# Layer 2 of a fused graph network: the pairs ordered by a list scheduler instead of hand-written steps

## The chip, the cores and the metric

One core of one Trainium2 chip runs the whole network in one launch. The metric is the device time of that launch in microseconds (us). The engines are named as in the profile: PE is the matmul engine and PEld its weight loads, DVE the vector engine, ACT the engine of activation functions, POOL the general-purpose engine, SP the queue that issues most DMA transfers.

## The reference, cut to what matters

Four graph layers run one after the other over 2708 nodes of 128 features with one dense 2708 x 2708 matrix `adj`. The change is in layer 2, which works on points of a hyperbolic ball:

```python
local_t = logmap(h[:, None, :], h[None, :, :])          # a vector for every pair i, j
scores = (h_t @ att_wl)[:, None] + (h_t @ att_wr)[None, :] + att_b[0]
adj_att = sigmoid(scores) * adj
support_t = jnp.einsum('ij,ijd->id', adj_att, local_t)  # sum over j
h = proj(expmap(support_t, h))
h = relu(logmap0(h))
x = _layernorm(x + proj(expmap0(h)))
```

`logmap` of a pair is a scalar factor times a fixed combination of the two points, so what must be made for every pair is one number: with a Gram product of the two points giving minus the hyperbolic cosine, less one, of their distance, the factor is the distance over its hyperbolic sine. This factor is the same for (i, j) and (j, i). It is multiplied by the sigmoid of the score and by `adj`, and the result is summed over j by matmuls.

## The kernel before, in words

Layers 0 and 1 come first, then layer 2's preparation, its stage of the pairs, its end, and layer 3. The change is inside the stage of the pairs.

The nodes are 22 tiles of 128 (the last has 20 rows), split in two halves of 11 tiles (`HT`). A `Pair` is one tile of neighbours j (the partitions) against one half of the nodes i (the columns: 1408 in half 0, 1300 in half 1). There are 44: `A` (half 0 with tiles of half 0), `B` (half 0 with tiles of half 1), `C` (half 1 with tiles of half 1), `D_` (half 1 with tiles of half 0). Since the factor is symmetric, A and C pairs work out only the columns from their own tile on (`dw` of them, "direct") and get the rest (`mw`) as transposes of earlier pairs' results, "mirrors". B pairs are all direct, and each stores its result in a DRAM table `f_tab`; D pairs are all mirrors, read from that table.

For a pair, the work on each engine is:

- PE: `gram` (L1386 in float32 and L1387 in bfloat16, up to 512 columns into one PSUM bank `ps`); `mirror` (L1449, transposes of 128 columns into a bank); `add_up` (L1464 into `accV`, three banks, and L1466 into `accO`, one bank).
- ACT: `clear` (L1396, relu out of the bank), `square` (L1400), `root` (L1404), `log` (L1414), `gate` (L1418, sigmoid). Root, logarithm and sigmoid lie in different function tables; each change of table is an ACT_TABLE_LOAD. Relu, square and copy run under any of them.
- DVE: `sinh` (L1407), `exp_d` (L1410), `over_sinh` (L1426), `gated_adj` (L1422), `times_f` (L1433), and the product with a mirror (L1450), each over the pair's columns.
- SP: `load` of the tile of `adj` (L1369), the store to `f_tab` (L1429), `load_f` from it (L1380 and L1381). POOL clears the diagonal (L1372).

All intermediate tiles lie in one `arena` of 264 cells of 128 columns. `taken` and `released` assign them in the order in which the program is written; a tile that is written into cells still being read waits for the reader. The four remaining PSUM banks rotate through one pool, `pg`, for grams and mirrors alike.

The instruction order on every engine is the written order (`tc.manual_schedule`). It comes from 14 hand-chosen `steps` of two to five pairs. In one step, in this order, the roots of the pairs `now`, the mirrors and last products of the pairs `done` (the step before), the first `add_up` and up to four clears of the pairs `after`, sinh and exp of `now`, the other add-ups alternating with the remaining grams and clears, then the logarithms, `gated_adj`, the loads and gates of `after`, `over_sinh`, and `load_f`. The first two grams of the step after next are placed at the end:

```python
for v in direct(now):
    v.log()
for v in now:
    v.gated_adj()
...
coming = [(v, a, b) for v in direct(at_step(step + 2)) for a, b in v.direct]
early = [v.gram(a, b) for v, a, b in coming[:2]]
```

After the last pair of a half, `accV` and `accO` are copied out by DVE and ACT in turn (L1478, L1479); the first half's sums are parked in DRAM (`v_tab`). Then the end of layer 2 and layer 3 start: transposes of the sums (L1623), and layer 3's matmuls over `adj` (L1726).

Of the kernel before, what the change touches and what calls it, by code (L numbers as in the profile page):

```python
# [35 lines left out]
def spans(start, stop, step):  # L36
    return [(a, min(a + step, stop)) for a in range(start, stop, step)]


@with_exitstack  # L40
def gnn_stack(ctx: ExitStack, tc: tile.TileContext, t, out: bass.AP):
# [975 lines left out]
    def layers_1_to_3(top, before_end=lambda: None):  # L1017
# [144 lines left out]
        with ExitStack() as l2:  # L1162
# [146 lines left out]
            with ExitStack() as att:  # L1309
                CELLS = 264  # L1310
                arena = att.enter_context(tc.tile_pool(name="arena", bufs=1)).tile([P, CELLS * P], F32, name="arena")
                pacc = att.enter_context(tc.tile_pool(name="ps_acc2", bufs=1, space=PSUM))
                pg = att.enter_context(tc.tile_pool(name="ps_g", bufs=4, space=PSUM))
                free = {k: -1 for k in range(CELLS)}
                clock = itertools.count()

                def taken(width):

                    n, runs = -(-width // P), []
                    for k in sorted(free):  # L1320
                        if runs and runs[-1][-1] == k - 1:
                            runs[-1].append(k)
                        else:
                            runs.append([k])
                    fits = [(len(r), max(free[k] for k in own), own[0]) for r in runs if len(r) >= n
                            for own in (r[:n], r[-n:])]
                    at = min(fits)[2]
                    for k in range(at, at + n):
                        del free[k]
                    return at  # L1330

                def released(cells):
                    free.update(dict.fromkeys(cells, next(clock)))

                class Pair:
# [4 lines left out]
                    def __init__(self, hf, j):  # L1340
                        self.hf, self.j, self.r = hf, j, rows[j]
                        self.c0, self.c1 = halves[hf]
                        self.w = self.c1 - self.c0
                        self.js = slice(j * P, j * P + self.r)
                        self.own_half = self.c0 <= j * P < self.c1
                        self.first = j - hf * HT if self.own_half else 0

                        self.mw = self.first * P if self.own_half else self.w if hf else 0
                        self.dw = self.w - self.mw
                        self.cells = {}  # L1350
                        self.direct, self.mirrors = spans(0, self.dw, BANK), spans(0, self.mw, BANK)
                        Pair.of[hf, j] = self

                    def new(self, name, width):
                        at = taken(width)
                        self.cells[name] = set(range(at, at + -(-width // P)))
                        return arena[:self.r, at * P:at * P + width]

                    def drop(self, name):
                        released(self.cells.pop(name))  # L1360

                    def drop_column(self, k):
                        cell = max(self.cells["f"]) - (HT - 1 - k)
                        self.cells["f"].discard(cell)
                        released([cell])

                    def load(self):
                        self.at = self.new("at", self.w)
                        nc.sync.dma_start(out=self.at, in_=adjT[self.js, self.c0:self.c1])  # L1369
                        if self.own_half:  # L1370
                            d = self.at[:, self.mw:self.mw + self.r]
                            nc.gpsimd.tensor_mul(d, d, off[:self.r, :self.r])  # L1372

                    def load_f(self):
                        if self.dw == 0:
                            at = taken(HW)
                            self.cells["f"] = set(range(at, at + HT))
                            f = self.fT = arena[:, at * P:at * P + HW].rearrange("p (k c) -> p k c", c=P)
                            k = HT - 1
                            nc.sync.dma_start(out=f[:, :k, :], in_=f_tab[:k, :, self.js].rearrange("k p c -> p k c"))  # L1380
                            nc.sync.dma_start(out=f[:rows[-1], k, :], in_=f_tab[k, :rows[-1], self.js])  # L1381

                    def gram(self, a, b):
                        ps = self.ps = pg.tile([P, BANK], F32, name="ps")[:self.r, :b - a]
                        c = slice(self.c0 + self.mw + a, self.c0 + self.mw + b)
                        nc.tensor.matmul(ps, XT[:, self.js], XT[:, c], start=True, stop=False)  # L1386
                        nc.tensor.matmul(ps, aux[0][:, self.js], aux[1][:, c], start=False, stop=True)  # L1387
                        return ps

                    def clear(self, a, b, ps, on_vector):  # L1390
                        if a == 0:
                            self.m = self.new("m", self.dw)
                        if on_vector:
                            nc.vector.tensor_scalar(self.m[:, a:b], ps, -1.0, 0.0, op0=ALU.mult, op1=ALU.max)
                        else:
                            nc.scalar.activation(self.m[:, a:b], ps, AF.Relu, scale=-1.0)  # L1396

                    def square(self):
                        self.u = self.new("u", self.dw)
                        nc.scalar.activation(self.u, self.m, AF.Square, bias=1.0)  # L1400

                    def root(self):
                        self.f = self.new("f", self.dw)
# [5 lines left out]
                    def exp_d(self):  # L1409
                        nc.vector.scalar_tensor_tensor(self.u, self.m, 1.0, self.u, op0=ALU.add, op1=ALU.add)  # L1410
                        self.drop("m")
# [4 lines left out]
                    def gate(self):  # L1416
                        self.w_ = self.new("w", self.w)
# [3 lines left out]
                    def gated_adj(self):  # L1421
                        nc.vector.tensor_mul(self.w_, self.w_, self.at)  # L1422
                        self.drop("at")

                    def over_sinh(self):
                        nc.vector.scalar_tensor_tensor(self.f, self.u, DMAX, self.f, op0=ALU.min, op1=ALU.mult)  # L1426
                        self.drop("u")
                        if not self.own_half:
                            nc.sync.dma_start(out=f_tab[self.j - HT, :self.r, :], in_=self.f)  # L1429

                    def times_f(self):
                        v = self.w_[:, self.mw:]
                        nc.vector.tensor_mul(v, v, self.f)  # L1433
                        if self.own_half:
# [4 lines left out]
                    def mirror(self, a, b):  # L1439
                        ps = pg.tile([P, BANK], F32, name="ps")[:self.r, :b - a]  # L1440
                        for c in range(a, b, P):
# [7 lines left out]
                            nc.tensor.transpose(ps[:, c - a:c - a + n], src, ident[:n, :n])  # L1449
                        nc.vector.tensor_tensor(self.w_[:, a:b], self.w_[:, a:b], ps, op=ALU.mult)  # L1450
                        if b == self.mw and self.own_half:
                            for k in range(self.first):
                                Pair.of[self.hf, self.hf * HT + k].drop_column(self.first)
                        elif b == self.mw:
                            self.drop("f")

                    def add_up(self, first, last):
                        if first:
                            Pair.acc = (pacc.tile([P, 3 * BANK], F32, name="accV"),
                                        pacc.tile([P, BANK], F32, name="accO"))  # L1460
                        accV, accO = Pair.acc
                        pieces = spans(0, self.w, BANK)
                        for a, b in pieces:
                            nc.tensor.matmul(accV[:, a:b], X[:self.r, self.j, :], self.w_[:, a:b], start=first, stop=last)  # L1464
                        for k, (a, b) in enumerate(pieces):
                            nc.tensor.matmul(accO[32 * k:32 * k + 1, :b - a], X0[:self.r, self.j:self.j + 1],  # L1466
                                             self.w_[:, a:b], start=first, stop=last)
                        self.drop("w")
                        if last:
                            if self.hf:  # L1470
                                VT = VT1
                            else:
                                at = taken(self.w)
                                VT = arena[:, at * P:at * P + self.w]
                                released(range(at, at + HT))
                            for k, (a, b) in enumerate(pieces):
                                copy = nc.scalar.copy if k % 2 else nc.vector.tensor_copy
                                copy(VT[:, a:b], accV[:, a:b])  # L1478
                                copy(V0T[32 * k:32 * k + 1, self.hf, :b - a], accO[32 * k:32 * k + 1, :b - a])  # L1479
                            if self.hf == 0:  # L1480
                                nc.sync.dma_start(out=v_tab, in_=VT)

                A, B = [Pair(0, j) for j in range(HT)], [Pair(0, j) for j in range(HT, NT)]
                C, D_ = [Pair(1, j) for j in range(HT, NT)], [Pair(1, j) for j in range(HT)]
                steps = [A[:2], A[2:5], A[5:7] + B[:1], A[7:8] + B[1:3], A[8:9] + B[3:5], A[9:10] + B[5:7],
                         A[10:] + B[7:9], B[9:], C[:2] + D_[:1], C[2:4] + D_[1:3], C[4:6] + D_[3:5], C[6:8] + D_[5:7],
                         C[8:] + D_[7:9], D_[9:]]
                order = [v for s in steps for v in s]
                assert len(order) == 2 * NT

                def direct(vs):
                    return [v for v in vs if v.dw]

                def at_step(n):
                    return steps[n] if 0 <= n < len(steps) else []

                with tc.manual_schedule():
                    early = []
                    for step in range(-1, len(steps) + 1):
                        now, after, done = at_step(step), at_step(step + 1), at_step(step - 1)  # L1500
                        adds = [functools.partial(v.add_up, n % NT == 0, n % NT == NT - 1)
                                for n, v in enumerate(order) if v in done]
# [326 lines left out]
```

## Time and profile before

| | |
|---|---|
| median of 3 runs | 1919.74 us (1918.43 to 1920.09) |
| the profiled execution | 1919.87 us, of which the span of instructions is 1918.0 us |
| PE busy over the span | 1620.9 us (85%) |
| DVE | 1441.5 us (75%) |
| ACT | 1041.9 us (54%) |
| POOL | 624.7 us (33%) |
| mean granted PE clock over the span | 0.919 |
| stage of the pairs | 1242.6 to 1620.0 us |
| in it: PE, DVE, ACT busy | 301.5, 252.6, 245.1 us of 377.4 us |
| in it: granted PE clock | 0.84 |

The busy times are sums over instructions; PE's are modelled and grow when the granted clock falls, so they are not an amount of work. In the lists of waits a line gives the engine and the line that waited, what it waited for, the total, the number of times and the longest. In the timeline a line gives start, duration, engine, line, output and inputs, count, and in brackets the idle time before it and what ended it. `arena` stands for every tile in the arena, so the line number tells which operation is meant.

### The profile page before, as it was taken

The numbers are of one execution on the slowest core, as the hardware profiler recorded it, in microseconds if no ns is written. First come the engines' busy times: TensorE is split into PE (matmuls) and PEld (weight loads), VectorE is DVE, ScalarE is ACT, GpSimd is POOL, SyncE is SP. The second block draws the span as 40 slices with busy tenths as digits, with TensorE's granted clock in tenths as the row PEclk, the third lists the DMA queues.
The fourth block names the chain that finished last, engine by engine and source line by source line (L and its number), as shares of the span: only waits on it lengthen the run. The fifth ranks groups of instructions, "written<-read, shape, count | busy, mean of one in ns | idle before, by whom it ended". The sixth has DMA issues, their size and how long they took to land.

```text
span 1918.0 us, 36613 instructions
## 1 busy us (share of the span) xinstructions
PE 1620.9 (85%) x14033; PEld 960.8 (50%) x14033; DVE 1441.5 (75%) x3615; ACT 1041.9 (54%) x1528; POOL 624.7 (33%) x426
## 2 busy tenths in 40 slices
PE   5899999999999999885699996678776888199995
PEld 5666666666666666664444443423222443044542
DVE  7899999999999999986588885757777764860104
ACT  3666667667666766654344443587777640440003
POOL 5667757766766776664100000000000000000000
PEclk8899999999999999997799998778897879599998
DMA  8756666665766666443044410022334543454331
GB/s 212 164 118 145 130 142 131 137 138 128 147 121 141 140 135 143 91 99 114 1 150 146 167 70 1 22 85 104 137 108 143 167 142 125 184 203 145 143 123 31
DMA packets 234896, 238.30 MB, mean 124 GB/s; under 512 B 28844, under 2 KB 219630, under 8 KB 228122
## 3 DMA queue, kind: packets, MB, share of 16 engines
q1 hardware_dynamic: 183670, 212.18, 35.7%
q0 software_dynamic: 51040, 23.68, 10.5%
q8 instruction: 112, 1.84, 0.4%
q14 instruction: 74, 0.61, 0.1%
HBM read 220.65 MB, written 15.15 MB: 123 GB/s over the span
## 4 chain that ended last, share of the span: by engine, by line
PE 41%; DVE 29%; POOL 8%; DMA 8%; issue 7%; ACT 6%; SPq 0%; DVEq 0%; ACTq 0%; POOLq 0%
PE acc L1726 10%; POOL far L782 8%; PE accV L1464 6%; PE lg L1099 5%; PE acc L1106 5%; DVE ix L778 5%; DMA far<-d_tab,ix 4%; DVE W L883 3%; DVE extra L796 2%; PE ps L1386 2%; PE accO L1466 2%; DVE o L740 2%; PE sl L818 2%; DVE S L708 2%; DVE dA L701 2%
## 5 line engine op out<-in xcount | busy, mean ns | idle before, releaser
L782 POOL DMA_INDIRECT far<-d_tab,ix x352 | 562.2, 1597 | 257.6 <-DVE W L883 112.1
L896 ACT ACTIVATE g<-sl 128x768 f32<-128x768 f32 x484 | 392.9, 812 | 257.9 <-PE sl L823 207.9
L818 PE MATMUL sl<-dA,S 124*128 124x153 f16 x4840 | 408.2, 232 | 10.4 <-DVE W L883 7.7
L818 PEld LDWEIGHTS <-S 124*128 124x128 f16 x4840 | 330.5, 98 | 79.8 <-issue 68.2
L834 PE MATMUL acc<-g,W 128*32 128x128 f32 x4840 | 205.5, 277 | 0.5 <-issue 0.5
L834 PEld LDWEIGHTS acc<-g,W 128*32 128x32 f32 x4840 | 140.6, 109 | 58.7 <-issue 55.5
L823 PE MATMUL sl<-s,same 50*128 50x384 f16 x968 | 161.9, 308 | 0.0
L883 DVE TENSOR_TENSOR W<-sl,own 128x150 f32<-128x150 f32 x484 | 143.2, 300 | 14.1 <-ACT g L896 13.5
L1464 PE MATMUL accV<-arena,X 128*128 128x512 f32 (+4 forms) x264 | 130.4, 636 | 20.9 <-DVE arena L1450 11.8
L1100 ACT ACTIVATE w<-lg,row_L_gnn_gate_bias 128x512 f32<-128x512 f32 (+1 forms) x132 | 83.4, 636 | 108.2 <-PE lg L1099 107.0
L708 DVE TENSOR_SCALAR S<-rk 124x1000 f16<-124x1000 bf16 (+1 forms) x330 | 133.9, 431 | 0.0
L778 DVE FIND_INDEX8 ix<-v,o 128x8 uint32<-128x2728 f32 x44 | 131.7, 2994 | 0.0
L1372 POOL TENSOR_TENSOR arena<-arena,off 128x128 f32<-128x128 f32 (+1 forms) x22 | 16.3, 741 | 344.2 <-DMA arena<-in_adjT 264.7
L1099 PE MATMUL lg<-qT,mT 128*128 128x512 f32 (+2 forms) x264 | 121.1, 547 | 3.6 <-ACT w L1100 3.1
L1106 PE MATMUL acc<-w,both 128*128 128x512 f32 (+2 forms) x264 | 121.2, 547 | 0.0
L796 DVE SCALAR_TENSOR_TENSOR extra<-far,v,extra 128x128 f32<-128x128 f32 x330 | 114.9, 348 | 6.3
L317 DVE TENSOR_TENSOR g<-ps,row_L_gnn_b 128x512 f32<-128x512 f32 (+2 forms) x14 | 8.0, 574 | 147.0 <-PE ps L315 147.0
L740 DVE SCALAR_TENSOR_TENSOR o<-ps,ar 128x496 f32<-128x496 f32 x132 | 82.4, 624 | 36.2 <-issue 20.8
L1726 PE MATMUL acc<-at,x 128*128 128x512 f32 (+2 forms) x156 | 66.2, 574 | 48.6 <-ACT x L247 48.6
L1101 DVE TENSOR_TENSOR w<-w,at 128x512 f32<-128x512 f32 (+1 forms) x132 | 82.6, 626 | 27.1 <-ACT w L1100 27.0
L1464 PEld LDWEIGHTS accV<-arena,X 128*128 128x128 f32 (+1 forms) x264 | 54.1, 219 | 89.0 <-issue 61.4
L747 DVE MAX8 cand<-o 128x8 f32<-128x248 f32 x242 | 90.4, 411 | 0.0
(360 smaller groups left out, 2524.9 us busy)
## 6 DMA issues: line engine op xcount, KB each, us to landing
at<-in_adjT SPq DMA_DIRECT2D x42, 1354.0 KB
ar<-in_adj SPq DMA_DIRECT2D x105, 248.0 KB
far<-s_tab SPq DMA_DIRECT2D x44, 512.0 KB
at<-in_adjT SPq DMA_DIRECT2D x42, 448.0 KB
arena<-in_adjT SPq DMA_DIRECT2D x21, 704.0 KB
arena<-in_adjT SPq DMA_DIRECT2D x21, 650.0 KB
held<-in_adjT SPq DMA_DIRECT2D x7, 1354.0 KB
f_tab<-arena SPq DMA_DIRECT2D x10, 704.0 KB
```

Of the source, the lines that this page charges most:

```text
L708: nc.vector.tensor_scalar(self.S[h][:, :n, :, k * RG:(k + 1) * RG], self.rk[h][:, :n, :LR].rearrange("p b (c i) -> p b c i", c=NC), EDGE + ...
L778: nc.vector.max_index(ix, self.v[:, n * 8:n * 8 + 8], self.o.rearrange("p b j -> p (b j)"))
L782: nc.gpsimd.indirect_dma_start(out=self.far[n][:, k, :], out_offset=None, in_=d_tab[:, :], in_offset=bass.IndirectOffsetOnAxis(ap=self.ix[ ...
L818: nc.tensor.matmul(group[c], self.S[h][:, n, c, :], dA[q][:, b, c, :], start=c % 3 == 0 and q == 0, stop=False)
L823: nc.tensor.matmul(out, same[p], self.s3[p, :e - a, :], start=False, stop=True)
L834: nc.tensor.matmul(self.acc[q:q + 32, k, :], W[:, c, :], g[:, c, :], start=b == 0 and k == 0, stop=ends)
L883: nc.vector.tensor_tensor(W[:, :, :RG].rearrange("p (k c) i -> p k c i", k=2), columns_of(sl, D, DA), own[:, None, None, :].to_broadcast([ ...
L896: nc.scalar.activation(g.rearrange("p (k c) d -> p k c d", k=2), columns_of(sl, 0, D), AF.Gelu, scale=1.0 / D_SCALE)
L1099: nc.tensor.matmul(lg, mT[:, j * P:j * P + r], qT[:, a:b], start=True, stop=True)
L1106: nc.tensor.matmul(acc[k], mrow[:rows[j], j, :], ws[j][:rows[j], a:b], start=j == 0, stop=j == NT - 1)
L1464: nc.tensor.matmul(accV[:, a:b], X[:self.r, self.j, :], self.w_[:, a:b], start=first, stop=last)
L1726: nc.tensor.matmul(acc[k], src[:rows[j], j, :], at[:rows[j], a:b], start=j == order[0], stop=j == order[-1])
```

## The change

The work of a pair is kept. What changes is how its order is made:

- Each operation of each pair becomes a `Step` with an engine, a cost in us, the steps it needs, a rank, and, where it applies, a group, how many groups ahead it may run, a function table, arena cells that it takes, and a kind of PSUM bank.
- `Plan.run` goes through an imagined time when the kernel is built: whenever an engine is free it takes the first of its steps, by rank, whose needs are met, writes its instruction, and moves on. On ACT the tables follow a fixed sequence (root, logarithm of a group, sigmoid of the next), and relu and square fill in.
- The four banks become one tile `banks4`, given out as they come free: at most three at a time for grams and two for mirrors.
- The 14 groups of pairs are others; D pairs begin in the seventh.
- An `add_up` may be cut between its pieces of 512 columns; mirrors and their products are separate steps.
- The sums of both halves are copied out by ACT alone.
- Arena cells are given back at the end that the plan gives to a step.

```diff
+class Plan:
+    LOAD, LATENCY = 1.28, 0.2
...
+        def can_start(s, earliest):
+            if any(a.end is None or a.end + self.LATENCY * (a.engine != s.engine) > now + 1e-9 for a in s.after):
+                return False
+            if s.ahead is not None and s.group - earliest > s.ahead:
+                return False
+            if s.bank and (not self.free_banks or self.kinds.get(s.bank[0], 0) >= s.bank[1]):
+                return False
+            if s.cells:
+                kept = sum(n for g, n in need.items() if g < s.group) if s.group > earliest else 0
+                return len(self.arena.free) >= s.cells + kept and self.arena.fit(s.cells) is not None
+            return True
+
+        while any(todo.values()):
+            earliest, moved = min((g for g, n in open_.items() if n), default=1 << 30), False
+            for e, steps in todo.items():
+                if free_at[e] > now + 1e-9:
+                    continue
+                if e == "ACT":
+                    while self.tables and not left.get(self.tables[0]):
+                        self.tables.pop(0)
+                    first = self.tables[0] if self.tables else None
+                    mine = [s for s in steps if s.table and s.table == first and can_start(s, earliest)]
+                    rest = [s for s in steps if not s.table and can_start(s, earliest)]
+                    late = first and first[0] == "log" and table != "log" and len(mine) < left[first]
+                    pick = (rest[:1] or mine[:1]) if late else (mine[:1] or rest[:1])
+                else:
+                    pick = [s for s in steps if can_start(s, earliest)][:1]
+                for s in pick:
+                    moved, s.end = True, now + s.cost
...
+                    s.emit()
...
-                pg = att.enter_context(tc.tile_pool(name="ps_g", bufs=4, space=PSUM))
+                banks4 = att.enter_context(tc.tile_pool(name="ps_g", bufs=1, space=PSUM)).tile([P, 4, BANK], F32, name="ps")
...
-                            for k, (a, b) in enumerate(pieces):
-                                copy = nc.scalar.copy if k % 2 else nc.vector.tensor_copy
-                                copy(VT[:, a:b], accV[:, a:b])
-                                copy(V0T[32 * k:32 * k + 1, self.hf, :b - a], accO[32 * k:32 * k + 1, :b - a])
+                        nc.scalar.copy(self.VT[:, a:b], accV[:, a:b])
+                        nc.scalar.copy(V0T[32 * k:32 * k + 1, self.hf, :b - a], accO[32 * k:32 * k + 1, :b - a])
...
-                steps = [A[:2], A[2:5], A[5:7] + B[:1], A[7:8] + B[1:3], A[8:9] + B[3:5], A[9:10] + B[5:7],
-                         A[10:] + B[7:9], B[9:], C[:2] + D_[:1], C[2:4] + D_[1:3], C[4:6] + D_[3:5], C[6:8] + D_[5:7],
-                         C[8:] + D_[7:9], D_[9:]]
+                together = [[named[v] for v in group.split()] for group in (
+                    "A0 A1 A2", "A3 A4 A5 B9", "A6 B1", "A7 A8 B3 B4", "B2 B6 B8", "A9 A10 B0 B7",
+                    "B5 B10 D0 D1", "C0 C1 D6", "C2 C3", "C4 D2 D3 D8", "C5 C6", "C7 D4 D5 D9",
+                    "C8 C9 D7 D10", "C10")]
+                plan = Plan(arena, 4, [("sigmoid", 0)] + [b for n in range(len(together)) for b in (
+                    ("root", n), ("log", n), ("sigmoid", n + 1))])
...
+                        at = one("SP", 3.2, v.load, ahead=1, cells=HT)
+                        if v.own_half:
+                            at = one("POOL", 0.8, v.clear_diagonal, [at])
+                        for a, b in spans(0, v.dw, BANK):
+                            fill, use, give = banked("gram", v.gram, v.clear, a, b)
+                            g = one("PE", 0.265 * (b - a) / P, fill, rank=0, ahead=2, bank=("gram", 3))
+                            last.append(one("ACT", 0.03 + 0.14 * (b - a) / P, use, [g], ahead=1,
+                                            cells=0 if a else dcells, then=give))
+                        if v.dw:
+                            s = one("ACT", looks, v.square, last, ahead=1, cells=dcells)
+                            s = one("ACT", 0.04 + 0.129 * t, v.root, [s], ahead=0, cells=dcells, table=("root", n))
+                            s = one("DVE", passes, v.sinh, [s], rank=1)
+                            s = one("DVE", passes, v.exp_d, [s], rank=0, then=functools.partial(v.drop, "m"))
+                            s = one("ACT", looks, v.log, [s], table=("log", n))
+                            s = over[v.hf, v.j] = one("DVE", passes, v.over_sinh, [s], rank=2,
+                                                      then=functools.partial(v.drop, "u"))
+                            if not v.own_half:
+                                kept.append(one("SP", 3.2, v.keep_f, [s]))
+                        s = one("ACT", 1.46, v.gate, ahead=1, cells=HT, table=("sigmoid", n))
+                        gated = one("DVE", 1.62, v.gated_adj, [s, at], rank=5, then=functools.partial(v.drop, "at"))
...
+                        if v.mw and not v.own_half:
+                            f = one("SP", 3.2, v.load_f, kept[:HT], ahead=0, cells=HT)
+                        for a, b in spans(0, v.mw, BANK):
+                            fill, use, give = banked("mirror", v.mirror, v.times_mirror, a, b)
...
+                            s = plan.add("PE", 0.13 * (b - a) / P, fill, [*fs, gated], rank=1, bank=("mirror", 2))
+                            last.append(plan.add("DVE", 0.02 + 0.168 * (b - a) / P, use, [s, gated], rank=3,
+                                                 then=given))
...
+                        for a, b in spans(0, v.w, BANK):
+                            before = plan.add("PE", 0.213 * (b - a) / P, functools.partial(v.add_up, a, b, *ends),
+                                              [*last, *outs, before], rank=2)
+                        before = plan.add("PE", 1.05, functools.partial(v.add_up_0, *ends), [before], rank=2,
+                                          then=functools.partial(v.drop, "w"))
```

## The prediction

> **What bounds the kernel now.** I read the shares of the engines over the stage of the pairs (1242.6 us, its first load, to 1620.0 us, the last copy of its sums: 377.4 us), then the waits of each engine in it, then one step in order of time. First the stretches: per line the width, then busy us of PE, PEld, DVE, ACT, POOL, and the granted clock.
>
> ```profile
> 1360.00:1400.00 40.00, 34.10 (x103) 11.53 (x102) 32.15 (x26) 27.57 (x32) 0.91 (x2) 0.91 0.35 127
> ...
> 1600.00:1620.00 20.00, 19.23 (x89) 8.32 (x87) 5.34 (x10) 2.19 (x4) 0.20 (x1) 1.00 0.06 16
> sum 378.00, PE 301.98 PEld 119.20 DVE 253.16 ACT 245.58 POOL 16.50; mean PE 25.17 PEld 9.93 DVE 21.10 ACT 20.46 POOL 1.37
> ```
>
> No engine is full: in 378 us DVE works 253, ACT 246, and PE's 302 contain stretches at a low clock. The end is lopsided: in the last 20 us PE works nearly alone, at full clock. Then who waits for whom (us, times, longest):
>
> ```profile
> DVE arena L1450 <- PE ps L1449: 49.0, 19, 13.2
> DVE arena L1426 <- ACT arena L1414: 44.8, 13, 7.8
> DVE arena L1407 <- ACT arena L1404: 22.9, 11, 12.5
> ...
> ACT arena L1396 <- PE ps L1387: 60.5, 25, 7.8
> ACT VT L1478 <- DVE VT L1478: 40.6, 1, 40.6
> ...
> PE ps L1449 <- DMA arena<-f_tab: 19.9, 3, 8.8
> ```
>
> The three wait in a circle: ACT for gram products, DVE for ACT's logarithms and for mirrors, PE for DVE. ACT's 40.6 is the tail. One step, in order of time:
>
> ```profile
> 1365.73 1.12 PE L1386 MATMUL ps<-XT 128*128 128x512 f32 x2
> 1366.79 0.38 PE L1387 MATMUL ps<-aux,aux 10*128 10x512 bf16 x1
> 1367.10 1.12 PE L1386 MATMUL ps<-XT 128*128 128x512 f32 x2
> ...
> 1375.10 1.28 ACT L1414 ACT_TABLE_LOAD   x1
> ...
> 1379.47 1.28 ACT L1418 ACT_TABLE_LOAD   x1
> ...
> 1382.03 4.07 PE L1464 MATMUL accV<-arena,X 128*128 128x512 f32 x6 [5.90 <-DVE arena L1450]
> ...
> 1389.47 2.63 PE L1464 MATMUL accV<-arena,X 128*128 128x512 f32 x6
> ...
> 1402.36 1.28 ACT L1414 ACT_TABLE_LOAD   x1
> ```
>
> From one logarithm table to the next, 27.3 us for three pairs. After the mirrors PE has nothing left that may start while ACT does logarithms and gates: 5.90 us empty, and the next add-up takes 4.07 where the following one takes 2.63. The granted clock is 0.50 at 1380 to 1384 and 1.00 at 1388.
>
> **What the Trainium skill says.** TensorE: Matmul & The Clock Gate, Part 1: activity releases the throttle, and about 3.4 us idle brings half rate back. The trace agrees: 0.50 after the 5.9 us gap, 1.00 throughout 1600 to 1620. The same page, Part 2, step 1: matmuls keep program order, only weight loads are pulled ahead; so a mirror whose data is late blocks the grams behind it (19.9 us above). ScalarE: Activation LUTs, What ACT_TABLE_LOAD costs: 1283 ns and a drain of about 1380. The trace has the 1283, but logarithms end at 1379.46 and the next load starts at 1379.47, so no drain; I use 1.28.
>
> **The change part by part.** The arithmetic per pair stays: the same grams, mirrors, add-ups, DVE passes, 44 loads of adjT, 11 stores to f_tab and 22 reads from it (two per D pair), 22 diagonal products on POOL. Only order, groups and banks move, and eight copies of sums go from DVE to ACT: DVE -4.7 us, ACT +4.7 (8 x 0.58). The changed kernel's order shows 42 table loads here instead of 40: ACT +2.6. So ACT about 253, DVE about 248.
>
> PE at full clock, from starts in the step above: a 512 gram, both matmuls, 1367.10 - 1365.73 = 1.37; a 384 gram 1.10 (the one at 1371.99; the next starts at 1373.09); that is 0.29 + 0.27 per 128 columns. An add-up is 2.56 + 0.96 = 3.52 in half 0 (from 1368.47 and 1371.03 in the same timeline), 2.38 + 0.96 = 3.34 in half 1; a transposed block 0.13 (22 in 2.88, at 1608). Over all: grams 88, add-ups 22 x 3.52 + 22 x 3.34 = 151, mirrors 231 x 0.13 = 30: **269**. The list of steps prices grams at 1.06 per 512: about 23 us too little in all. PE, not DVE or ACT, will be the fullest engine.
>
> By step or group I add PE (grams, mirrors and add-ups of its pairs), DVE (passes 0.06 + 0.142 per 128 columns, gated product 1.62 or 1.5, mirror product 0.02 + 0.168 per 128) and ACT (clears 0.59 per 512, squares and logarithms 1.38 per 1408, roots 1.46, gates 1.46 or 1.37, three tables), and take the largest. Before, steps 0 to 13: 18.0, 21.1, 20.2, 22.1, 21.6, 21.1, 20.6, 18.5, 18.5, 22.5, 21.6, 20.8, 24.9, 9.5 = 281; it took 377, so 96 us are waits and cold clock. After: groups 0 to 6 24.2, 27.7, 15.4, 26.5, 25.8, 25.6, 24.3 = 169.5 (PE 160, DVE 163, ACT 162: all three even); groups 7 to 13 18.5, 14.8, 20.4, 11.8, 19.7, 19.9, 5.4 = 110.5 (PE 108, DVE 90, ACT 85). Again 280: regrouping removes no work. What goes is the waiting:
> - PE's hole per step. Grams may run two groups ahead, in up to three banks, and add-ups drop in between piece by piece, so PE has work while ACT does logarithms. The hole with its cold restart costs 5.9 + 1.5 = 7.4 per step; I allow 0.7 for each of 14 groups, since ends of one engine still start another: 10 us.
> - The tail. D pairs are spread over groups 6 to 12, and only C10 stands last (PE 5.0); the 40.6 us in which ACT had no work shrink to a drain of 6 copies x 0.58 = 3.5 us.
> - The start: a table, three gates 4.4, clears and square of A0 3.0: 8.7 us until the first root, as exposed as before (first DVE pass after 12.5 us).
> - The reads of f_tab. They are moved to after the last stores (group 6), behind up to six loads on SP's queue. The step costs each DMA 3.2 us; measured from issue to the mirror, 6.68 and 8.49. They stand in five bunches; the first of each can be 3.3 late, 16 us, bounded below by 0 where PE is still behind its plan. I take half: 8. Behind a late mirror stand grams and add-ups on PE; ACT's clears and DVE's mirror products wait for those.
> - Loads of adjT come earlier and up to ten together; hidden by the group between load and use. Without that cover 4.8 us (1242.6 to the diagonal product at 1247.4), once. POOL's product rides on the same cover. WAR waits on arena cells are on SP only, as now. The f_tab stores wait only for over_sinh and delay loads behind them: nothing, while a load has a group's lead.
> - Banks: one tile of four where four rotated. Mirrors now keep at most two, grams three. From 0 to 0.6 us (one clear) per gram; I take 0, as PE has add-ups to put in between.
>
> Sum: 8.7 + 280 + 10 + 8 + 3.5 = 310, against 377.4: **-67 us**. On the profiled execution, 1919.87 us (span 1918.0), that is 1853; the median of the runs is 1919.74, 0.13 lower, so the forecast stays 1853. Layer 3 starts at the last copy and moves along rigidly.
>
> **The rivals.**
> - Everything overlaps (a): PE at full clock nearly without a gap. 269 + 8.7 + 3.5 and half the allowances, 9: 290, so 1833. For it: plan costs agree with the rows except grams and DMA. Against: in groups 0 to 6 all three engines are within 2%, so each delay of one shows.
> - Half is given back (b): with grams under-priced, PE lags where ACT expects them; the hole only falls to 2.5 per group (35), reads cost 15: 8.7 + 280 + 35 + 15 + 3.5 = 342, so 1885. For it: ACT's 60.5 us for grams.
> - Slower (c): SP's order puts each read behind loads that wait for cells, and all 11 reads stand bare before PE, 6.7 each, with the cold restart 1.5: 90 in place of 8, so 392 and 1935. It turns slower from 75 us, 6.8 per D pair. Against: reads are issued in threes, and mirrors of C pairs and add-ups stand between.
> - The change does not do what it says (d): the banks in one tile are waited for as a whole, so each of 68 grams waits for the clear before it, 0.6: 41 on top of the 310, 351, so 1894.
>
> **How the numbers follow.** The main case 0.60, (a) 0.15, (b) 0.17, (c) 0.04, (d) 0.03, and 0.01 for no change. Main alone 1842 to 1874 (the 21.5 us of allowances and drain halved or doubled). The range 1828 to 1890 takes in (a) and (b), the bounds of reads (0 to 16) and holes, and leaves out (c) and (d). About 0.2% is what can be told from no change; faster 0.95, same 0.01, slower 0.04.
>
> **What would show it.** Right: the stage takes about 310 us; PE busy over 85% of it, clock over 0.90; ACT's wait for grams under 30 us and DVE's for logarithms under 15; no stretch over 10 us where ACT is idle before the end. The read step is wrong if PE waits over 20 us for f_tab; the hole step if the clock stays near 0.85. The forecast is wrong altogether if the stage takes over 347 us, or if PE is the idlest of the three.

## The result, and the profile after

The changed kernel takes 1904.72 us (median of 4 runs, 1904.10 to 1905.26) against 1919.09 us before (4 runs beside them): ratio 0.9925, interval 0.9908 to 0.9942. That is 14.4 us faster, where the forecast said 67, and outside the range 1828 to 1890. The lines of the stage moved down by 104 to 113: gram L1386 and L1387 are now L1499 and L1500, clear L1396 is L1505, mirror L1449 is L1554, its product L1450 is L1557, add-up L1464 is L1571, the copy of the sums L1478 is L1582.

First the stage of the pairs as a whole, 1241.7 us (first load) to 1602.5 us (last copy), and its first 42 us. The columns are width, busy PE, PEld, DVE, ACT, POOL, granted clock (then the DMA share and GB/s).

```profile
1241.70:1602.50 360.80, 304.96 (x983) 112.22 (x983) 247.68 (x246) 253.31 (x273) 21.79 (x23) 0.85 0.38 125
...
1242.00:1262.00 20.00, 11.26 (x14) 2.90 (x14) 8.12 (x5) 14.45 (x15) 3.51 (x5) 0.58 0.63 206
1262.00:1284.00 22.00, 17.82 (x26) 4.90 (x25) 5.83 (x4) 10.07 (x13) 1.12 (x1) 0.50 0.10 43
```

The same 42 us in the kernel before:

```profile
1242.00:1262.00 20.00, 12.45 (x28) 3.75 (x26) 7.35 (x6) 17.89 (x24) 0.91 (x2) 0.75 0.20 72
1262.00:1284.00 22.00, 17.36 (x35) 5.76 (x34) 15.32 (x13) 19.47 (x21) 2.71 (x3) 0.61 0.29 99
```

The stage takes 360.8 us instead of 377.4. DVE has 247.7 us of work and ACT 253.3, as the sums said (248 and 253). But PE's 305 are no fewer than before's 301, the clock is 0.85 against 0.84, and in the first 42 us DVE works 14 us (23 before) and PE runs at about half clock (0.58 and 0.50; before 0.75 and 0.61). Who waits for whom, in the stage (us, times, longest; three engines, three answers):

```profile
PE ps L1499 <- ACT arena L1505: 26.5, 30, 6.4
PE ps L1554 <- DVE arena L1557: 13.2, 13, 3.7
...
ACT arena L1505 <- PE ps L1500: 48.9, 27, 3.2
ACT VT L1582 <- PE accV L1571: 25.1, 1, 25.1
ACT arena L1505 <- PE ps L1554: 14.4, 9, 4.1
...
DVE arena L1557 <- PE ps L1554: 19.6, 15, 2.8
...
DVE arena L1557 <- PE ps L1500: 15.7, 5, 5.3
DVE arena L1557 <- ACT arena L1505: 12.0, 2, 8.4
```

DVE's wait for logarithms (was 44.8) is down to 19.6, and no line of PE waiting for f_tab is left. But there are waits here that the arithmetic doesn't have. L1557 multiplies by a mirror, and it waits for L1500, the second matmul of a gram, 15.7 us, and for a clear on ACT, 12.0 us. L1505 clears a gram, and it waits for L1554, a mirror, 14.4 us. No datum goes from one to the other; they share nothing but the tile `banks4`. The start shows how it works, in order of time:

```profile
1247.40 0.57 ACT L1505 ACTIVATE arena<-ps 128x512 f32<-128x512 f32 x1
1248.03 2.07 PE L1499 MATMUL ps<-XT 128*128 128x512 f32 x2 [6.41 <-ACT arena L1505]
1250.03 0.60 PE L1500 MATMUL ps<-aux,aux 10*128 10x512 bf16 x1
1250.67 0.98 ACT L1505 ACTIVATE arena<-ps 128x512 f32<-128x512 f32 x2 [2.70 <-PE ps L1500]
1251.70 2.08 PE L1499 MATMUL ps<-XT 128*128 128x512 f32 x2 [1.07 <-ACT arena L1505]
```

Three grams were done before 1242. The fourth goes to the fourth bank, which no pair has used, and yet waits until the first clear is over (1247.97). The second and third clears read banks filled long before, and yet wait until the fourth gram is over (1250.63). Each engine waits for the last access of the other to the tile as a whole, so PE and ACT alternate.

### The profile page after: what moved, and what is told of

Its sections match the earlier page's. It is cut to its first block, busy times and chain, and to the rows that moved or that the text cites. A ratio compares the mean times of both kernels' runs of the same rounds, so it can differ in the third digit from the quotient of the medians.

```text
span 1903.5 us, 36624 instructions
## 1 busy us (share of the span) xinstructions
PE 1626.2 (85%) x14033; PEld 955.4 (50%) x14033; DVE 1436.1 (75%) x3607; ACT 1052.1 (55%) x1538; POOL 630.8 (33%) x426
## 4 chain that ended last, share of the span: by engine, by line
PE 43%; DVE 28%; POOL 8%; issue 7%; ACT 7%; DMA 5%; DVEq 0%; SPq 0%; ACTq 0%; POOLq 0%
PE acc L1843 10%; POOL far L914 8%; PE lg L1231 5%; PE acc L1238 5%; PE accV L1571 5%; DVE ix L910 5%; PE ps L1499 4%; DMA far<-d_tab,ix 3%; DVE W L1015 3%; PE sl L950 3%; DVE extra L928 2%; DVE o L872 2%; DVE S L840 2%; PE accO L1575 2%; DVE dA L833 1%
## 5 line engine op out<-in xcount | busy, mean ns | idle before, releaser
L1486 POOL TENSOR_TENSOR arena<-arena,off 128x128 f32<-128x128 f32 (+1 forms) x22 | 21.6, 982 | 351.1 <-DMA arena<-in_adjT 321.3
L1571 PE MATMUL accV<-arena,X 128*128 128x512 f32 (+4 forms) x264 | 124.7, 592 | 6.5 <-DVE arena L1537 6.5
L1499 PE MATMUL ps<-XT 128*128 128x512 f32 (+8 forms) x150 | 90.4, 691 | 32.2 <-ACT arena L1505 26.5
```

The costliest lines, as they stand in the source:

```text
L1571: nc.tensor.matmul(Pair.acc[0][:, a:b], X[:self.r, self.j, :], self.w_[:, a:b], start=first, stop=last)
```

## The experiments

Theory T: these waits hold for the whole tile `banks4`, and they took the gain (rival (d) of the prediction). Rival U: the order of the list itself makes PE and ACT alternate. All times are medians of 4 runs, with 7 runs of the kernel before on the same chip: one chip for e1 to e4, a second for e5 to e7, a third for e8. Across chips the ratios to before are what to compare.

**Four tiles instead of one** (e1_tiles). Order, groups and bank numbers stay.

```diff
-banks4 = att.enter_context(tc.tile_pool(name="ps_g", bufs=1, space=PSUM)).tile([P, 4, BANK], F32, name="ps")
+pg = att.enter_context(tc.tile_pool(name="ps_g", bufs=1, space=PSUM))
+banks4 = [pg.tile([P, BANK], F32, name=f"ps{k}") for k in range(4)]
...
-banks4[:self.r, bank, :b - a]
+banks4[bank][:self.r, :b - a]
```

> The changed kernel with its four PSUM banks as four tiles instead of one tile of four banks; order and groups untouched. Theory T: in the changed kernel every gram waits for the last clear written before it, whatever its bank, and every clear for the last gram (48.9 + 26.5 us of such waits, and PE at half clock for the first 42 us). With a tile for each bank these waits go, and the forecast's sum applies: stage about 310 us, time 1840 to 1874. Rival U: the list's order itself makes PE and ACT alternate (three gram banks, PE priced too cheap), the tile is innocent: 1898 to 1906, waits of ACT for grams still 40 to 60 us.

Measured: 1852.83 us, ratio to before 0.966 (0.9644 to 0.9677), where the changed kernel had 0.9925. That is 51.9 us less than the changed kernel (about 51 by the ratios) and inside T's range; U is out. The stage, here from its first load at 1239.7 us to its last copy at 1550.5 us, then the waits:

```profile
1239.70:1550.50 310.80, 282.83 (x980) 108.10 (x980) 247.12 (x246) 251.51 (x273) 19.79 (x23) 0.91 0.44 146
```

```profile
PE ps L1555 <- DVE arena L1558: 7.9, 6, 3.1
PE ps L1500 <- ACT arena L1506: 6.4, 1, 6.4
...
ACT VT L1583 <- PE accV L1572: 23.9, 1, 23.9
ACT arena L1506 <- PE ps L1501: 12.4, 16, 1.9
...
DVE arena L1558 <- PE ps L1555: 20.3, 19, 3.1
DVE arena L1534 <- ACT arena L1523: 9.9, 6, 5.5
```

(Lines are one further down: gram L1500 and L1501, clear L1506, mirror L1555, product L1558.) The three pairs of lines named above that share no data are gone; the 26.5 us in 30 waits of grams for clears became 6.4 us in one; ACT's 48.9 became 12.4. The one that is left is needed: the fourth gram is now done at 1239.6, and it is the fifth, which fills the first bank again, that waits for the first clear. Of the 50.0 us by which the stage got shorter, 27.9 are PE's idle time (360.80 - 304.96 = 55.84, against 310.80 - 282.83 = 27.97), and 22.1 are PE's busy time for the same matmuls, at a clock of 0.91 for 0.85.

By part, 14.7 us are saved before the first add-up (34.1 for 48.8 us), 26.1 from there to the first copy of half 0's sums (173.2 for 199.3), and 9.2 after it (103.5 for 112.7). In the kernel before these parts take 30.7, 198.4 and 148.3 us: with one tile the changed kernel reaches half 0's sums 19 us later in the stage than before, and wins only after them. The same place in order of time:

```profile
1250.09 2.08 PE L1500 MATMUL ps<-XT 128*128 128x512 f32 x2
1250.98 1.34 ACT L1506 ACTIVATE arena<-ps 128x512 f32<-128x512 f32 x3
1252.10 0.60 PE L1501 MATMUL ps<-aux,aux 10*128 10x512 bf16 x1
```

ACT now empties banks while PE fills another. The Trainium skill, PSUM — Partial Sum Buffer, PSUM bank collisions raise a hardware error, says that a guard by bank is enough and that accesses of two engines to different banks run clean at the same time; this run agrees (a gram at 1250.09 to 1252.17, clears at 1250.98 to 1252.32).

**One tile in the kernel before** (e2_before_one). The rotating pool becomes one tile whose banks are taken in turn; nothing else.

```diff
-pg = att.enter_context(tc.tile_pool(name="ps_g", bufs=4, space=PSUM))
+banks4 = att.enter_context(tc.tile_pool(name="ps_g", bufs=1, space=PSUM)).tile([P, 4, BANK], F32, name="ps")
+turn = itertools.cycle(range(4))
...
-pg.tile([P, BANK], F32, name="ps")[:self.r, :b - a]
+banks4[:self.r, next(turn), :b - a]
```

> The kernel before with only its four rotating bank tiles made into one tile of four banks, taken in turn; steps untouched. Theory T: it gets slower, by up to 0.6 us for each of 68 grams and 69 mirror pieces that would have run ahead: 1930 to 1990. Rival U: within 4 us of before, 1915 to 1924.

Measured: 2008.75 us, ratio 1.0479 (1.0447 to 1.0512), 91 us slower, beyond the upper end of T's 1990. The waits of DVE, PE and ACT (lines one further down than before):

```profile
DVE arena L1451 <- PE ps L1450: 95.8, 55, 18.3
...
PE ps L1450 <- DVE arena L1451: 64.4, 53, 5.7
PE ps L1387 <- ACT arena L1397: 38.9, 43, 5.8
...
ACT arena L1397 <- PE ps L1388: 101.2, 48, 5.1
```

Before, DVE's and ACT's two waits were 49.0 and 60.5 us, and PE's were these:

```profile
PE ps L1449 <- DVE arena L1450: 19.6, 7, 5.1
PE ps L1386 <- ACT arena L1396: 7.5, 2, 6.5
```

Mirror pieces and their products (L1450, L1451) now wait for each other over 50 times. The tile by itself costs in both orders, 91 us in the written one and 52 in the list's. That the written order puts all mirrors of a step one after the other, where the list puts other work between, may be why it suffers more; this was not tried.

**Two tiles of two banks** (e5_two_tiles).

```diff
+twos = [pg.tile([P, 2, BANK], F32, name=f"ps{k}") for k in range(2)]
+banks4 = [twos[k // 2][:, k % 2, :] for k in range(4)]
```

> The changed kernel with its four banks as two tiles of two banks; order and groups untouched. Theory T (a wait holds for a whole tile, so only banks of one tile hold each other up): in between the changed kernel, 1904.7, and four tiles, 1852.8: 1862 to 1892. Rival: banks 0 and 1 are mostly filled and emptied together, so half the tile is as bad as all of it (1897 to 1907) or as free as four (1850 to 1858).

Measured: 1861.33 us, ratio 0.9702 (0.9673 to 0.9731). In between, as T says, but a little under its range: one split gives back 43 of the 52 us. The time alone hardly tells it from four tiles, measured on another chip: the intervals of the ratios meet (0.9673 and 0.9677). The waits do tell: those between operations that share no data are still there, smaller (gram L1502, clear L1507, product L1559):

```profile
DVE arena L1559 <- PE ps L1502: 10.9, 5, 3.9
...
DVE arena L1559 <- ACT arena L1507: 2.9, 2, 1.5
```

**PE's prices** (e3_costs). Four tiles, and two edits together: the plan reckons with the gram and add-up times of the trace, and the clears of a pair are kept in their order, which the other prices would not do by themselves.

```diff
-g = one("PE", 0.265 * (b - a) / P, fill, rank=0, ahead=2, bank=("gram", 3))
-last.append(one("ACT", 0.03 + 0.14 * (b - a) / P, use, [g], ahead=1,
+g = one("PE", 0.29 + 0.27 * (b - a) / P, fill, rank=0, ahead=2, bank=("gram", 3))
+last.append(one("ACT", 0.03 + 0.14 * (b - a) / P, use, [g, *last[-1:]], ahead=1,
...
-before = plan.add("PE", 0.213 * (b - a) / P, functools.partial(v.add_up, a, b, *ends),
+before = plan.add("PE", 0.233 * (b - a) / P, functools.partial(v.add_up, a, b, *ends),
...
-before = plan.add("PE", 1.05, functools.partial(v.add_up_0, *ends), [before], rank=2,
+before = plan.add("PE", 0.96, functools.partial(v.add_up_0, *ends), [before], rank=2,
```

> Four tiles as in the first, and the plan's PE costs set to what the trace of before shows: gram 0.29 + 0.27 per 128 columns for 0.265 per 128, add-up 0.233 per 128 and 0.96 for 0.213 and 1.05; the clears of one pair keep their order. Theory T: the wrong prices cost the rest of ACT's waits for grams: 3 to 12 us faster than the first of these runs. Rival: list and chip drift apart anyway, the prices do not matter: within 2 us of it, either way.

Measured: 1846.76 us (1845.76 to 1847.88), ratio 0.9633 (0.9617 to 0.9649); 6.1 us less than e1_tiles, whose runs on the same chip lie at 1849.39 to 1854.59. The two edits together matter a little, a third of a per cent; the prices alone were not tried. ACT's wait for grams falls to 6.1 us in 7 waits. From 1440 to 1540 us PE has no gap:

```profile
1440.00:1480.00 40.00, 40.00 (x163) 17.44 (x163) 37.97 (x44) 37.10 (x42) 3.26 (x3) 0.95 0.64 207
1480.00:1520.00 40.00, 40.00 (x206) 20.68 (x205) 32.78 (x55) 22.96 (x29) 1.13 (x3) 1.00 0.50 157
1520.00:1540.00 20.00, 20.00 (x77) 7.10 (x76) 1.52 (x3) 0.00 (x0) 0.00 (x0) 1.00 0.00 1
```

**The old steps as groups** (e4_oldgroups: four tiles; e6_costs_oldgroups: PE's prices as measured besides). Only the strings of `together` change.

```diff
-"A0 A1 A2", "A3 A4 A5 B9", "A6 B1", "A7 A8 B3 B4", "B2 B6 B8", "A9 A10 B0 B7",
-"B5 B10 D0 D1", "C0 C1 D6", "C2 C3", "C4 D2 D3 D8", "C5 C6", "C7 D4 D5 D9",
-"C8 C9 D7 D10", "C10"
+"A0 A1", "A2 A3 A4", "A5 A6 B0", "A7 B1 B2", "A8 B3 B4", "A9 B5 B6", "A10 B7 B8",
+"B9 B10", "C0 C1 D0", "C2 C3 D1 D2", "C4 C5 D3 D4", "C6 C7 D5 D6",
+"C8 C9 C10 D7 D8", "D9 D10"
```

> Four tiles and the list scheduler, but the 14 groups are the old steps (D pairs last, D9 D10 at the end). Theory T with the forecast's tail: the end is again PE alone, 10 to 30 us slower than the first of these runs. Rival: the list fills the tail by itself, groups are worth under 4 us.

> Four tiles, PE's prices as measured, and the old steps as groups. If groups are worth nothing with the list, as the fourth run said (1853.6 to 1852.8), then 1844 to 1851, within 4 us of the new groups at 1846.8. Rival: the new groups were chosen for the old prices, so the old ones win by 5 us or more; or they lose by 5 or more once PE is priced right.

Measured: 1853.57 us (0.9671, 0.9655 to 0.9687) beside e1_tiles' 1852.83; with the prices 1846.57 us (0.9627, 0.9596 to 0.9657) beside e3_costs' 1846.76. Both times no difference that can be told, so the 10 to 30 us that the forecast's tail would cost are not there. Of e4_oldgroups, ACT's longest wait:

```profile
ACT VT L1583 <- PE accV L1572: 39.1, 1, 39.1
```

ACT stands idle for 39.1 us before the end, as long as in the kernel before (40.6), and the kernel is not slower for it.

**Two gram banks instead of three** (e7_gram2), on top of e3_costs: `bank=("gram", 3)` becomes `bank=("gram", 2)`.

> Four tiles, PE's prices as measured, but at most two banks at a time for grams instead of three. If letting grams run ahead through the banks is what fills PE while ACT does logarithms: 8 to 25 us slower than 1846.8. Rival: two banks are enough because a clear takes 0.6 us and a gram 1.37: within 3 us.

Measured: 1852.14 us, ratio 0.9648 (0.9621 to 0.9675). By the medians 5.4 us over e3_costs, by the ratios to before, taken on two chips, not to be told apart; it lies between both expectations. ACT's wait for grams is 17.2 us in 16 waits instead of 6.1, so the third bank does keep grams ahead, but it is worth little.

**Eleven groups** (e8_eleven), on top of e3_costs.

```diff
+"A0 A1 A2", "A3 A4 A5 B9", "A6 A7 B1 B3", "A8 B4 B2 B6", "A9 B8 B0 B7",
+"A10 B5 B10 D0 D1", "C0 C1 D6", "C2 C3 C4 D2 D3", "C5 C6 D8 D4 D5", "C7 C8 C9 D9 D7",
+"C10 D10"
```

> As the third run (four tiles, PE's prices as measured, 1846.8), with the 44 pairs in 11 groups instead of 14: 33 changes of ACT's table instead of 42, 11.5 us less of ACT, 3.9 of it in half 0. If ACT paces half 0: 3 to 8 us faster. Rival: PE, full from 1440 to 1540 in that run, paces the whole, and ACT's saving only lengthens its idle tail: within 3 us; or larger groups wait for arena cells: slower by over 3 us.

Measured: 1851.09 us (1845.06 to 1853.72), ratio 0.9642 (0.9621 to 0.9663): nothing gained. Over the stage ACT's busy time fell from 249.8 us in e3_costs to 237.6, its idle tail grew from 29.9 to 34.6, and PE's busy time stayed (283.7 and 283.9). So ACT's work does not pace the stage, which fits PE as the pace. Whether the larger groups also wait for arena cells stays open: by the medians 4.3 us are lost, by the ratios, on two chips, nothing that can be told.

## Why the prediction was wrong, point by point

- **The step that failed: the banks.** "From 0 to 0.6 us (one clear) per gram; I take 0, as PE has add-ups to put in between." It was 52 us, 1904.7 to 1852.8 (51 by the ratios). The reason given for 0 fails twice. At the start there is no add-up to put in between: 42 us pass with 14 us of DVE work, and 14.7 us are lost before the first add-up. And the wait goes in both directions and across kinds: a clear waits for a later gram (ACT 48.9), a mirror product for a gram or a clear (DVE 15.7 + 12.0), which the bound of one clear per gram leaves out. With the lower clock (22 us of it) this makes 52 where (d) had 41, for 68 grams; there are 75.
- **The rival (d)** named the mechanism, and its 1894 is near the 1904.7, but it had 0.03 of the chance and was left outside the range. What spoke for it was in the diff: the one edit that merges four objects into one, priced by a single sentence.
- **The rest of the sum held in total, with luck in its parts.** With the tile split, the stage takes 310.8 us for the 310 and the kernel 1852.8 for the 1853. The sum had 41 us on top of PE's 269. Measured are 14 for the clock (282.8 us busy at 0.91 for the 269 at full clock), for which the sum had no term of its own, and 28 of idle PE. The reads of f_tab, 8 in the sum, are in no wait of PE; that PE is by then behind its plan is the likely reason. What follows the stage did not move along rigidly: it takes 298.0 us before, 301.0 in the changed kernel, 300.1 in e1_tiles.
- **The tail and the groups.** "The 40.6 us in which ACT had no work shrink to a drain." They stay 23.9 in e1_tiles and 39.1 with the old groups, at the same time. ACT's idle end never was the cost; PE's work was, and the other grouping does not change it. "Regrouping removes no work" was right; the regrouping is worth nothing that can be measured.
- **PE the fullest engine** was right: 282.8 of 310.8 us, and in e3_costs 100 us without a gap. Right too was that grams are priced too low: correcting it, with the order of the clears, gives 6.1 us. The drain of six copies, 3.5 in the sum, took 3.4 in e1_tiles (1547.09 to 1550.51).
- **Rivals (b) and (c)**: the prices, with the order of the clears, are worth 6.1 us, not the 32 that (b) adds to the sum, and no read stands bare before PE. Rival (a), 1833, was not reached by any run; PE's cold start stands against it (0.50 until 1262.6 in e1_tiles).
- **The signs that were named** tell it by themselves: ACT's wait for grams 48.9 us, over 30; the clock 0.85, under 0.90; the stage 360.8 us, over 347. The last said that the forecast was wrong altogether, the first where.

## What to carry to other kernels

When an edit gathers buffers that rotated into one object, look at who waits for whom on that object before anything else: a wait between two operations that exchange no data is its mark, and here one tile per bank undid it. An order that keeps several results in flight is worth only what the waits allow; here the same order gave 14 us with one tile and about 65 with four. Of the list's parts only the groups were tried apart; how the 65 us divide among the order itself, the add-ups cut in pieces and the copies on ACT alone is open. Where three engines have nearly equal sums, the idle time of one at the end is no measure of what can be won: ask which engine's sum the stage cannot go below.

## What was not expected of the hardware and its program

The waits follow the PSUM tile, not the bank: with one tile of four banks each access waits for the other engine's last access to any of them, with two tiles most of this is gone, with four all of it. The arena, one SBUF tile of 264 cells, is not treated so: in the changed kernel ACT's root writes cells at 1254.37 to 1255.84 while a product of DVE (1253.18 to 1254.80) writes others. Why the two differ was not tried.

And a wait costs twice on PE: of the 50.0 us by which the stage shrank, 22.1 were no waiting but the same matmuls at a lower granted clock. That clock is 0.50 from 1245.1 to 1296.2 with one tile, and from 1242.2 to 1262.6 with four. The Trainium skill, TensorE: Matmul & The Clock Gate, Part 1, gives about 3.4 us of idle PE for the fall to half rate and about 3.4 us of sustained activity for the way back. In the changed kernel the fall fits: PE stops at 1241.6, and 3.4 us later the clock is down. In the kernel before it came sooner: PE stops at 1376.1, and over 1378 to 1380 the clock is 0.54. The way back does not fit: in e1_tiles one gram follows the other without a gap for 16.5 us, and the clock stays at half.

```profile
1246.10:1262.60 16.50, 16.50 (x23) 4.67 (x23) 12.92 (x9) 14.32 (x18) 3.54 (x5) 0.50 0.66 218
```

Why grams at half clock do not bring the full one sooner was not tried.
